# Graph products in quarters of TensorE's array, and whole transposes over all 128 rows in the place of halves

## The chip, the cores and the metric

The kernel runs on one core of one Trainium2 chip. The metric is the device time of one execution in microseconds, the median of several runs. TensorE (PE in the profile) does matmuls into PSUM; VectorE (DVE), ScalarE (ACT) and GpSimd (POOL) do the rest, and SyncE (SP) issues most DMAs. PE's array has 128 rows and 128 columns. A matmul on 64 rows or 64 columns may use a part of the array, and parts that don't overlap may work side by side. All data is fp32, and the profile shows two PE instructions for one fp32 matmul and one for a transpose.

## The reference: what is computed

`x` has 128 graphs of 64 nodes with 256 features; `adj` is one 64x64 adjacency matrix for all of them. Four graph layers follow one another, each as `x = layernorm(x + layer(x))`:

- Layer 0: the normalised adjacency is multiplied with every graph (`einsum('nm,bmd->bnd', A_hat, features)`), then two linear maps with batch norms and a relu.
- Layer 1: a Chebyshev-like product with a matrix from the adjacency and its largest eigenvalue, a linear map with layer norm and relu, attention with 4 heads inside each graph masked by the adjacency, and a feed-forward part with gelu.
- Layer 2: two graph convolutions, each `relu(einsum('ts,bsh->bth', adj, x @ W + b))`, then four LSTM passes over windows of 1 to 4 nodes, each pass writing its last state back into the nodes.
- Layer 3: graph attention with one score vector, a softmax over neighbours and a product with the values.

## The kernel before, in words

**Tiling.** The 128 graphs are cut into 16 blocks of 8 graphs. A block is one tile of 128 partitions x 1024 elements. In the token-major layout (`tm`) a partition holds one node of one graph of a pair, two graphs fill the 128 partitions, and four such pairs (`t`) with 256 features each fill the row. In the feature-major layout (`fm`) a partition is a feature, in two chunks `c` of 128, and the row holds 512 tokens. A PSUM stock `PS` has 4 such tiles of two banks each; `mem` is a stock of SBUF tiles that are taken and given back.

**Helpers on PE around the change.** `halves` is the pair of row ranges 0 to 63 and 64 to 127.

- `aggregate` (L334, matmuls at L340) is the graph product. Since the adjacency of a pair of graphs is block diagonal, it multiplies each half of the rows alone with its own 64x64 block `mT[h, h]`. The data is the stationary operand: 64 rows x 128 columns, which gives 128 features on the PSUM partitions and 64 tokens along the row. One call has 2 x 4 x 2 = 16 matmuls. Its result is feature-major.
- `to_fm` (L348) and `to_tm` (L356) turn a block from one layout to the other by PE transposes of half the rows each (L354, L361), 16 for a block. The attention weights are transposed the same way at L870.
- `part` (L320) gives each row half its own PSUM bank, so a 128-token column group lies in two places 512 elements apart. `joined` and `runs` (L324, L328) are views of PSUM and SBUF that put the two together when ScalarE or VectorE copy them out:

```
def part(ps, s, g):
    return ps[:, s * TB + g * N : s * TB + (g + 1) * N]
```

**Where they are called.** `aggregate` runs once per block in `first_block` (layer 0, L570), once in `block` (layer 1, L763) and twice in `gcn_block` (layer 2, L1317 and L1339): 64 calls. `to_tm` runs in `end_block` (L748) and in `last_block` (layer 3, L1480), `to_fm` twice in `block` (L783, L909) and once in `last_block` (L1491); with L870 that makes 96 sets of transposes. Copies out of PSUM follow each: L574 and L765, L1323, L1342 for the graph products; L751, L786, L874, L913, L1484 and L1499 for the transposes. The attention scores (L836) and the weighted values (L884) in `block` use quarters of the array, 64 rows x 64 columns, in both kernels.

**Order of the work.** The program is written by a planner, `flow` (L130). Each block's work is a generator that yields steps, `step(engine, us, ps, sl)`: the engine, a planned duration, and how many PSUM tiles and SBUF slots it takes. `flow` keeps a clock per engine and always emits the step that could begin soonest by those planned durations. So a planned duration changes no instruction, but it can change the order in which all blocks' instructions are written to each engine's queue. Within an engine the queue is worked off in that order. Up to 6 blocks of a stream are in flight, and in the middle of the run the layers overlap: LSTM units, convolutions and attention blocks of different graphs are interleaved on PE.

Of the kernel before, what the change touches and what calls it, by code (L numbers as in the profile page):

```python
# [10 lines left out]
AF = mybir.ActivationFunctionType  # L11
ALU = mybir.AluOpType
# [3 lines left out]
P = 128  # L16
B, N, D = 128, 64, 256
NBLK = 16
TB = 512
NT = 4  # L20
# [13 lines left out]
def kernel(ctx: ExitStack, tc: tile.TileContext, a: dict, out: bass.AP):  # L34
    nc = tc.nc
    V, S, G, T = nc.vector, nc.scalar, nc.gpsimd, nc.tensor
# [185 lines left out]
    H = [fm(s) for s in Hs]  # L222
# [3 lines left out]
    PS = Stock([ctile([P, NT * D], f"ps{j}", psp) for j in range(4)])  # L226
    mem = Stock([ctile([P, NT * D], f"t{j}", big) for j in range(TEMPS)])
# [15 lines left out]
    halves = slice(0, N), slice(N, P)  # L243
    for s in range(2):
        h = halves[s]
# [8 lines left out]
    ident = ctile([P, P], "ident")  # L254
# [65 lines left out]
    def part(ps, s, g):  # L320

        return ps[:, s * TB + g * N : s * TB + (g + 1) * N]

    def joined(ps, n=2 * NT):  # L324

        return ps.rearrange("p (s g e) -> p g s e", s=2, e=N)[:, :n]

    def runs(ap):  # L328

        if len(ap.shape) == 2:  # L330
            return ap.rearrange("p (g s e) -> p g s e", s=2, e=N)
        return ap.rearrange("p t (c s e) -> p (t c) s e", s=2, e=N)

    def aggregate(ps, y, mT):  # L334


        for c in range(2):
            for t in range(NT):
                for s, h in enumerate(halves):
                    T.matmul(  # L340
                        part(ps, s, c * NT + t),
                        y[h, t, c * P : (c + 1) * P],
                        mT[h, h],
                        start=True,
                        stop=True,
                    )

    def to_fm(ps, y):  # L348

        n = y.shape[1]  # L350
        for c in range(2):
            for t in range(n):
                for s, h in enumerate(halves):
                    T.transpose(part(ps, s, c * n + t), y[h, t, c * P : (c + 1) * P], ident[h, h])  # L354

    def to_tm(ps, yT):  # L356

        for t in range(yT.shape[2] // P):
            for c in range(2):
                for s, h in enumerate(halves):  # L360
                    T.transpose(part(ps, s, 2 * t + c), yT[h, c, t * P : (t + 1) * P], ident[h, h])  # L361

    def mm_fm(ps, w, yT, nk, off=0):

# [43 lines left out]
    with c0:  # L408
# [151 lines left out]
        def first_block(i):  # L560
            if i >= len(early):
                yield step("Q", 6.0, sl=1)
                xs = mem.take()
                nc.sync.dma_start(tm(mem[xs]), x_blk[i])
            else:
                xs = early[i]
            yield step("T", 0.95, ps=1, sl=1)
            ps = PS.take()
            ag = mem.take()
            aggregate(PS[ps], tm(mem[xs]), AhT)  # L570
            mem.give(xs)
            yield step("V", 1.25, ps=-1)
            aggT = fm(mem[ag])
            V.tensor_copy(runs(mem[ag]), joined(PS[ps]))  # L574
            PS.give(ps)
            for hf in range(2):
                dst = fm(Xs[i]) if hf == 0 else H[i]
                yield step("T", 3.45, ps=1)
                ps = PS.take()
                mm_fm(fm(PS[ps]), W1T, aggT, 2, off=2 * hf)  # L580
                if hf:
                    mem.give(ag)
                yield step("S", 1.3, ps=-1, waits=hf == 1)
# [136 lines left out]
        g2c = ctile([P, 2], "g2c")  # L720
        be2c = ctile([P, 2], "be2c")
# [14 lines left out]
    def end_block(i):  # L736
        x = X[i]
        yield step("Q", 6.0, sl=1)
        xin = mem.take()
        nc.sync.dma_start(tm(mem[xin]), x_blk[i])  # L740
        yield step("S", 1.4)
        for c in range(2):
            S.activation(
                H[i][:, c, :], H[i][:, c, :], AF.Identity, scale=sc2[:, c : c + 1], bias=sh2[:, c : c + 1]
            )
        yield step("T", 0.5, ps=1)
        ps = PS.take()
        to_tm(PS[ps], H[i])  # L748
        mark("h", i)
        yield step("V", 1.25, ps=-1)  # L750
        V.tensor_tensor(runs(x), joined(PS[ps]), runs(mem[xin]), ALU.add)  # L751
        PS.give(ps)
        mem.give(xin)
        yield from ln_steps_act(x)
        mark("end", i)

    def block(i):
        x = X[i]
        mark("begun", i)
        yield step("T", 0.95, ps=1, sl=1)  # L760
        ps = PS.take()
        s_xp = mem.take()
        aggregate(PS[ps], x, LnT)  # L763
# [4 lines left out]
        ps = PS.take()  # L768
# [4 lines left out]
        y = tm(mem[s_y])  # L773
# [3 lines left out]
        yield step("V", 1.25)  # L777
        V.scalar_tensor_tensor(y, y, 0.0, x, ALU.max, ALU.add)

        yield step("T", 0.5, ps=1, sl=1)  # L780
        ps = PS.take()
        s_x1 = mem.take()
        to_fm(PS[ps], y)  # L783
        yield step("S", 1.05, ps=-1)
        x1T = fm(mem[s_x1])
        S.copy(runs(mem[s_x1]), joined(PS[ps]))  # L786
        PS.give(ps)
        qk = []
        for w in (Wq, Wk):
            yield step("T", 3.45, ps=1, sl=1)  # L790
            ps = PS.take()
# [12 lines left out]
        ps = PS.take()  # L804
        s_v = mem.take()
        pv = PS[ps].rearrange("p (b u e) -> p b u e", b=8, u=2)
        for b in range(8):
            for r in range(2):
                for k in range(2):
# [4 lines left out]
                        start=(k == 0),  # L814
                        stop=(k == 1),
# [8 lines left out]
        G.tensor_tensor(y, y, row["bo"], ALU.add)  # L824


        yield step("T", 1.8, ps=1, sl=1)
        ps = PS.take()
        s_e = mem.take()
        pq = PS[ps].rearrange("p (r g m) -> p r g m", r=2, g=8)  # L830
        for t in range(NT):
            for u in range(2):
                for s in range(2):
                    b = 2 * t + s
                    for r in range(2):
# [4 lines left out]
                            start=True,  # L840
                            stop=True,
# [4 lines left out]
        e = mem[s_e].rearrange("p (g r m) -> p g r m", g=8, r=2)  # L846
# [15 lines left out]
        G.tensor_tensor(em, em, bc_last(sums, N), ALU.mult)  # L862


        yield step("T", 0.5, ps=1, sl=1)
        ps = PS.take()
        s_a = mem.take()
        for g in range(8):
            for s, h in enumerate(halves):
                T.transpose(part(PS[ps], s, g), mem[s_e][h, g * P : (g + 1) * P], ident[h, h])  # L870
        mem.give(s_e)
        yield step("S", 1.05, ps=-1)
        aT = mem[s_a].rearrange("p (g m) -> p g m", g=8)
        S.copy(runs(mem[s_a]), joined(PS[ps]))  # L874
        PS.give(ps)
        yield step("T", 1.3, ps=1, sl=1)
        ps = PS.take()
        s_o = mem.take()
        po = fm(PS[ps])
        for b in range(8):  # L880
            t, s = b // 2, b % 2
            for u in range(2):
                for r in range(2):
# [4 lines left out]
                        start=True,  # L888
                        stop=True,
# [7 lines left out]
        ps = PS.take()  # L897
# [5 lines left out]
        yield from ln_steps(y)  # L903


        yield step("T", 0.5, ps=1, sl=1)
        ps = PS.take()
        s_x2 = mem.take()
        to_fm(PS[ps], y)  # L909
        yield step("S", 1.4, ps=-1)  # L910
        x2T = fm(mem[s_x2])
        for c in range(2):
            S.activation(  # L913
                runs(mem[s_x2])[:, c * NT : (c + 1) * NT],
                joined(PS[ps])[:, c * NT : (c + 1) * NT],
                AF.Identity,
                scale=g2c[:, c : c + 1],
                bias=be2c[:, c : c + 1],
            )
        PS.give(ps)  # L920
        yield step("G", 4.7, waits=False)
# [3 lines left out]
        for hf in range(2):  # L925
            yield step("T", 3.45, ps=1, sl=1)
            ps = PS.take()
# [5 lines left out]
            for c in range(2):  # L933
                f = 2 * hf + c
# [7 lines left out]
        ps = PS.take()  # L942
        for t in range(NT):
            for k in range(4):
# [4 lines left out]
                    start=(k == 0),  # L949
                    stop=(k == 3),  # L950
# [360 lines left out]
        mem.give(s_cell)  # L1311

    def gcn_block(i):
        yield step("T", 0.95, ps=1, sl=1)
        ps = PS.take()
        s_a = mem.take()
        aggregate(PS[ps], X[i], bdAT)  # L1317
# [15 lines left out]
        PS.give(ps)  # L1333
        yield step("S", 1.05)
        S.activation(mem[s_h1], mem[s_h1], AF.Relu)
        yield step("T", 0.95, ps=1, sl=1)
        ps = PS.take()
        s_a = mem.take()
        aggregate(PS[ps], h1, bdAT)  # L1339
# [123 lines left out]
    def last_block(i, t0=0, nt=NT):  # L1463
# [9 lines left out]
        for c in range(2):  # L1473
# [1 line left out]
                hb[:, c, :].rearrange("p (b n) -> p b n", n=N),  # L1475
                hT_block(i)[:, c, :, 2 * t0 : 2 * (t0 + nt)].rearrange("p n b -> p b n"),
            )
        yield step("T", 0.5 * r, ps=1)
        ps = PS.take()
        to_tm(PS[ps], hb)  # L1480
        mem.give(s_h)
        mark("read", i)
        yield step("V", 0.1 + 1.2 * r, ps=-1)
        V.tensor_tensor(runs(x), joined(PS[ps], 2 * nt), runs(x), ALU.add)  # L1484
        PS.give(ps)
        yield from ln_steps_act(x)

        yield step("T", 0.5 * r, ps=1, sl=1)
        ps = PS.take()
        s_xT = mem.take()  # L1490
        to_fm(PS[ps], x)  # L1491


        yield step("S", 0.2 + 0.95 * r, ps=-1)
        xT = mem[s_xT][:, : 2 * nt * P]
        into = xT.rearrange("p (g f e) -> p g f e", f=4, e=N)
        pairs = joined(PS[ps], 2 * nt).rearrange("p (g f) s e -> p g f s e", f=2)
        for s, f in enumerate((slice(0, 4, 3), slice(1, 3))):
            S.copy(into[:, :, f], pairs[:, :, :, s])  # L1499
        xT = xT.rearrange("p (c k) -> p c k", c=2)  # L1500
        PS.give(ps)
        s12 = sm.tile([P, NT, 2], F32, tag="s12", name="s12")
        for t in range(0, nt, 2):
# [241 lines left out]
```

## Time and profile before

| what | value |
|---|---|
| median of 3 runs | 2440.89 us (2439.8 to 2445.77) |
| the profiled execution's own time | 2446.48 us |
| its span, first to last instruction | 2444.7 us |
| mean granted clock of TensorE | 0.979 |
| PE busy | 2323.0 us, 15636 instructions |
| PE weight loads busy | 1789.4 us |
| VectorE busy | 1255.6 us |
| ScalarE busy | 1185.4 us |
| GpSimd busy | 591.0 us |
| graph products (L340), 2048 PE instructions | 133.8 us busy |
| half transposes (L354, L361, L870), 1536 PE instructions | 73.9 us busy |

A busy time is the union of the instructions' spans on an engine. Matmuls overlap in the pipeline, so what a group costs PE is read from the start of its first instruction to the start of the next group, not from its durations. "Slot" is used below in that sense. A group's line is that of the helper, so L340 stands for all graph products.

### The profile page before, as it was taken

How to read it: one execution, taken by the hardware profiler on the slowest of the kernel's cores; microseconds unless marked ns; L12 is line 12 of the kernel's file. 1: busy time of each engine (PE TensorE's matmuls, PEld its weight loads, DVE VectorE, ACT ScalarE, POOL GpSimd, SP SyncE). 2: the span in 40 equal slices, each digit the busy share in tenths (PEclk: the TensorE clock that was granted, in tenths of full speed). 3: DMA queues.
4: the chain of work that ended last, by engine and by line, in shares of the span. 5: the costliest groups of instructions: out<-in, count | busy, mean ns of one | idle time of the engine just before them, and what ended most of it. 6: DMA issues, size and time to landing. Idle time of an engine off the chain costs nothing. (4 is left out here: it accounts for less than half of the span.)

```text
span 2444.7 us, 38027 instructions
## 1 busy us (share of the span) xinstructions
PE 2323.0 (95%) x15636; PEld 1789.4 (73%) x15636; DVE 1255.6 (51%) x2904; ACT 1185.4 (48%) x2168; POOL 591.0 (24%) x441
## 2 busy tenths in 40 slices
PE   8999878999999999999999999999999999989997
PEld 5548655767666667566677888899999888877775
DVE  4557577656447538266334344344444445455445
ACT  1248553444444343444444444444445554567676
POOL 0002134323224223233222222222221222122112
PEclk9999889999999999999999999999999999999998
DMA  5100301100000000001000000000001000101101
GB/s 154 52 1 1 106 26 40 36 9 10 1 10 10 18 10 10 1 18 44 9 27 1 27 18 1 1 18 1 1 1 35 1 10 9 35 27 44 52 18 53
DMA packets 42622, 57.74 MB, mean 24 GB/s; under 512 B 6224, under 2 KB 35536, under 8 KB 42448
## 3 DMA queue, kind: packets, MB, share of 16 engines
q1 hardware_dynamic: 41344, 54.22, 6.8%
q8 instruction: 123, 2.02, 0.4%
q10 hardware_dynamic: 1104, 1.08, 0.1%
q14 instruction: 51, 0.42, 0.1%
HBM read 38.52 MB, written 16.78 MB: 23 GB/s over the span
## 5 line engine op out<-in xcount | busy, mean ns | idle before, releaser
L1134 PE MATMUL ps<-x,x 128*128 128x256 f32 x864 | 212.9, 381 | 1.6 <-DVE x L1193 1.0
L1134 PEld LDWEIGHTS ps<-x,x 128*128 128x128 f32 x864 | 160.6, 190 | 25.2 <-issue 2.0
L1134 PE MATMUL ps<-t,x 128*128 128x256 f32 x704 | 170.0, 380 | 0.0
L314 ACT ACTIVATE x<-x,ln_nm,ln_rs 128x256 f32<-128x256 f32 x188 | 99.6, 592 | 122.9 <-DVE ln_nm L311 122.9
L1134 PEld LDWEIGHTS ps<-t,x 128*128 128x128 f32 x704 | 132.9, 190 | 18.9 <-issue 0.8
L308 POOL TENSOR_TENSOR ln_rs<-ln_rs,neghalf 128x4 f32<-128x4 f32 (+1 forms) x72 | 69.9, 970 | 213.0 <-DVE ln_rs L274 200.7
L367 PE MATMUL ps<-t,W1T 128*128 128x512 f32 x256 | 116.5, 603 | 0.0
L1210 ACT ACTIVATE t<-t,bih 128x512 f32<-128x512 f32 (+2 forms) x63 | 40.4, 641 | 105.7 <-DVE t L1200 101.0
L294 POOL TENSOR_TENSOR ln_rs<-ln_rs,neghalf 128x4 f32<-128x4 f32 x32 | 36.6, 1143 | 224.4 <-DVE ln_rs L274 224.4
L1062 PE MATMUL ps<-h,wL 128*128 128x192 f32 (+2 forms) x456 | 90.4, 352 | 0.0
L1062 PE MATMUL ps<-h,x 128*128 128x256 f32 x384 | 86.8, 380 | 1.5 <-ACT t L1074 1.5
L1193 DVE COPY t<-ps 128x256 f32<-128x256 f32 (+2 forms) x63 | 23.4, 371 | 123.9 <-PE ps L1134 123.9
L272 DVE BATCH_NORM_STATS2 ln_st<-x 128x6 f32<-128x256 f32 x224 | 85.4, 403 | 0.4
L367 PEld LDWEIGHTS ps<-t,W1T 128*128 128x128 f32 x256 | 47.4, 194 | 49.4 <-issue 49.4
L1062 PEld LDWEIGHTS ps<-h,wL 128*128 128x128 f32 x456 | 70.1, 190 | 16.8 <-issue 15.8
L1062 PEld LDWEIGHTS ps<-h,x 128*128 128x128 f32 x384 | 72.7, 190 | 12.3 <-ACT t L1074 1.6
L1074 ACT ACTIVATE t<-ps,bih 128x512 f32<-128x512 f32 (+3 forms) x108 | 63.6, 639 | 34.3 <-PE ps L1062 34.2
L1062 PE MATMUL ps<-t,wL 128*128 128x512 f32 x168 | 73.7, 594 | 1.3 <-ACT t L1360 0.7
L1074 ACT ACTIVATE x<-ps,bih 128x512 f32<-128x512 f32 (+3 forms) x84 | 48.9, 634 | 52.3 <-PE ps L1062 52.1
L273 DVE BATCH_NORM_AGGREGATE ln_mv<-ln_st 128x2 f32<-128x6 f32 x448 | 71.6, 167 | 0.0
L1210 ACT ACTIVATE x<-x,bih 128x512 f32<-128x512 f32 (+2 forms) x64 | 41.8, 653 | 57.6 <-DVE x L1200 57.4
L1062 PE MATMUL ps<-x,wL 128*128 128x512 f32 x144 | 62.9, 593 | 0.0
(712 smaller groups left out, 5760.6 us busy)
## 6 DMA issues: line engine op xcount, KB each, us to landing
t<-in_x_dram SPq DMA_DIRECT2D x26, 512.0 KB, 4.2
xd<-x SPq DMA_DIRECT2D x16, 512.0 KB, 2.6
x<-xd SPq DMA_DIRECT2D x6, 512.0 KB, 3.4
out_dram<-x SPq DMA_DIRECT2D x6, 512.0 KB, 3.0
h<-in_x_dram SPq DMA_DIRECT2D x5, 512.0 KB, 3.9
wL<-in_L_gnn_Wih_dram SPq DMA_DIRECT2D x2, 1024.0 KB, 5.1
x<-in_L_gnn_Whh_dram SPq DMA_DIRECT2D x2, 1024.0 KB, 6.2
t<-xd SPq DMA_DIRECT2D x4, 512.0 KB, 3.6
```

Of the source, the lines that this page charges most:

```text
L272: V.bn_stats(st[:, t, :], y[:, t, :])
L273: V.bn_aggr(mv[:, t, :], st[:, t, :])
L294: G.tensor_tensor(rs, rs, neghalf[:, :NT], ALU.pow)
L308: G.tensor_tensor(rs, rs, neghalf[:, :n], ALU.pow)
L314: S.activation(y[:, t, :], y[:, t, :], AF.Identity, scale=rs[:, t : t + 1], bias=nm[:, t : t + 1])
L367: T.matmul(ps[:, c, :], w[:, k, (off + c) * P : (off + c + 1) * P], yT[:, k, :], start=(k == 0), stop=(k == nk - 1),)
L1062: T.matmul(spread(fm(PS[ps])[:, j, :n], q), WL[p][0][:, k, m], x_of(0, q)[:, k], start=(k == 0), stop=(k == 1),)
L1074: S.activation(of(sl)[:, j], fm(PS[ps])[:, j, :n], AF.Tanh if g == 2 else AF.Sigmoid, bias=bias(g, c))
L1134: T.matmul(dst, WS[p][name](k, g), y[:, k], start=first and k == 0, stop=k == 1, skip_group_check=not first)
L1193: V.tensor_copy(y[:, 1, :], v[:, 0, :])
L1210: S.activation(of(act[g])[:, 0], of(act[g])[:, 0], f, bias=bias(g, 0))
```

## The change

`aggregate` splits each matmul in two by its stationary columns: 64 rows x 64 columns, which write 64 PSUM partitions each, at the same PSUM places as before, so its results are copied out with the same views. One call has 32 matmuls in the place of 16.

`to_fm`, `to_tm` and the attention transposes work on all 128 rows and 128 columns at once with the whole identity: 8 transposes for a block in the place of 16. Their results lie contiguous in PSUM, so the copies that follow use plain views. In `last_block` the swap of the two halves of every second pair, which the old views held, becomes three copies in the place of two.

The planned durations of the graph products go from 0.95 to 1.15 us, of the scores from 1.8 to 1.15, of the weighted values from 1.3 to 1.15, and of a set of transposes from 0.5 to 0.9; that of the copy in `last_block` goes from 0.2 + 0.95 r to 0.3 + 1.1 r, where r is the part of a block that is worked on.

```diff
         for c in range(2):
             for t in range(NT):
-                for s, h in enumerate(halves):
-                    T.matmul(
-                        part(ps, s, c * NT + t),
-                        y[h, t, c * P : (c + 1) * P],
-                        mT[h, h],
...
+                for f, to in enumerate(halves):
+                    for s, h in enumerate(halves):
+                        T.matmul(
+                            part(ps, s, c * NT + t)[to],
+                            y[h, t, c * P + f * N : c * P + (f + 1) * N],
+                            mT[h, h],
...
     def to_fm(ps, y):
-        n = y.shape[1]
         for c in range(2):
-            for t in range(n):
-                for s, h in enumerate(halves):
-                    T.transpose(part(ps, s, c * n + t), y[h, t, c * P : (c + 1) * P], ident[h, h])
+            for t in range(y.shape[1]):
+                T.transpose(ps[:, c, t * P : (t + 1) * P], y[:, t, c * P : (c + 1) * P], ident)
 
     def to_tm(ps, yT):
-        for t in range(yT.shape[2] // P):
+        for t in range(ps.shape[1]):
             for c in range(2):
-                for s, h in enumerate(halves):
-                    T.transpose(part(ps, s, 2 * t + c), yT[h, c, t * P : (t + 1) * P], ident[h, h])
+                T.transpose(ps[:, t, c * P : (c + 1) * P], yT[:, c, t * P : (t + 1) * P], ident)
...
-            yield step("T", 0.95, ps=1, sl=1)
+            yield step("T", 1.15, ps=1, sl=1)
             ps = PS.take()
             ag = mem.take()
             aggregate(PS[ps], tm(mem[xs]), AhT)
...
-        yield step("T", 0.5, ps=1)
-        ps = PS.take()
-        to_tm(PS[ps], H[i])
+        yield step("T", 0.9, ps=1)
+        ps = PS.take()
+        to_tm(tm(PS[ps]), H[i])
         mark("h", i)
         yield step("V", 1.25, ps=-1)
-        V.tensor_tensor(runs(x), joined(PS[ps]), runs(mem[xin]), ALU.add)
+        V.tensor_tensor(x, tm(PS[ps]), tm(mem[xin]), ALU.add)
...
-        S.copy(runs(mem[s_x1]), joined(PS[ps]))
+        S.copy(mem[s_x1], PS[ps])
...
-        yield step("T", 1.8, ps=1, sl=1)
+        yield step("T", 1.15, ps=1, sl=1)
...
         for g in range(8):
-            for s, h in enumerate(halves):
-                T.transpose(part(PS[ps], s, g), mem[s_e][h, g * P : (g + 1) * P], ident[h, h])
+            T.transpose(PS[ps][:, g * P : (g + 1) * P], mem[s_e][:, g * P : (g + 1) * P], ident)
...
-        yield step("T", 1.3, ps=1, sl=1)
+        yield step("T", 1.15, ps=1, sl=1)
...
-        yield step("S", 0.2 + 0.95 * r, ps=-1)
-        xT = mem[s_xT][:, : 2 * nt * P]
-        into = xT.rearrange("p (g f e) -> p g f e", f=4, e=N)
-        pairs = joined(PS[ps], 2 * nt).rearrange("p (g f) s e -> p g f s e", f=2)
-        for s, f in enumerate((slice(0, 4, 3), slice(1, 3))):
-            S.copy(into[:, :, f], pairs[:, :, :, s])
-        xT = xT.rearrange("p (c k) -> p c k", c=2)
+        yield step("S", 0.3 + 1.1 * r, ps=-1)
+        xT = fm(mem[s_xT])[:, :, : nt * P]
+        pairs, into = (ap.rearrange("p c (u e k) -> p c u e k", e=2, k=P) for ap in (px, xT))
+        S.copy(into[:, :, :, 0], pairs[:, :, :, 0])
+        for h in range(2):
+            S.copy(into[:, :, :, 1, halves[1 - h]], pairs[:, :, :, 1, halves[h]])
```

More of the change, by code (lines that the diff above doesn't have):

```diff
@@ L338, in aggregate @@
             for t in range(NT):
-                for s, h in enumerate(halves):
-                    T.matmul(
-                        part(ps, s, c * NT + t),
-                        y[h, t, c * P : (c + 1) * P],
-                        mT[h, h],
-                        start=True,
-                        stop=True,
-                    )
+                for f, to in enumerate(halves):
[4 more added lines that the diff above has]
+                            mT[h, h],
+                            start=True,
+                            stop=True,
+                        )
     def to_fm(ps, y):
-        n = y.shape[1]
         for c in range(2):
-            for t in range(n):
-                for s, h in enumerate(halves):
-                    T.transpose(part(ps, s, c * n + t), y[h, t, c * P : (c + 1) * P], ident[h, h])
+            for t in range(y.shape[1]):
+                T.transpose(ps[:, c, t * P : (t + 1) * P], y[:, t, c * P : (c + 1) * P], ident)
     def to_tm(ps, yT):
-        for t in range(yT.shape[2] // P):
+        for t in range(ps.shape[1]):
             for c in range(2):
-                for s, h in enumerate(halves):
-                    T.transpose(part(ps, s, 2 * t + c), yT[h, c, t * P : (t + 1) * P], ident[h, h])
+                T.transpose(ps[:, t, c * P : (c + 1) * P], yT[:, c, t * P : (t + 1) * P], ident)
     def mm_fm(ps, w, yT, nk, off=0):
@@ L759, in block @@
         mark("begun", i)
-        yield step("T", 0.95, ps=1, sl=1)
+        yield step("T", 1.15, ps=1, sl=1)
         ps = PS.take()
@@ L778, in block @@
         V.scalar_tensor_tensor(y, y, 0.0, x, ALU.max, ALU.add)
-        yield step("T", 0.5, ps=1, sl=1)
+        yield step("T", 0.9, ps=1, sl=1)
         ps = PS.take()
         s_x1 = mem.take()
-        to_fm(PS[ps], y)
+        to_fm(fm(PS[ps]), y)
         yield step("S", 1.05, ps=-1)
         x1T = fm(mem[s_x1])
-        S.copy(runs(mem[s_x1]), joined(PS[ps]))
+        S.copy(mem[s_x1], PS[ps])
         PS.give(ps)
@@ L862, in block @@
         G.tensor_tensor(em, em, bc_last(sums, N), ALU.mult)
-        yield step("T", 0.5, ps=1, sl=1)
+        yield step("T", 0.9, ps=1, sl=1)
         ps = PS.take()
@@ L873, in block @@
         aT = mem[s_a].rearrange("p (g m) -> p g m", g=8)
-        S.copy(runs(mem[s_a]), joined(PS[ps]))
+        S.copy(mem[s_a], PS[ps])
         PS.give(ps)
-        yield step("T", 1.3, ps=1, sl=1)
+        yield step("T", 1.15, ps=1, sl=1)
         ps = PS.take()
@@ L903, in block @@
         yield from ln_steps(y)
-        yield step("T", 0.5, ps=1, sl=1)
+        yield step("T", 0.9, ps=1, sl=1)
         ps = PS.take()
         s_x2 = mem.take()
-        to_fm(PS[ps], y)
+        to_fm(fm(PS[ps]), y)
         yield step("S", 1.4, ps=-1)
@@ L913, in block @@
             S.activation(
[L914 to L918, printed above, removed]
+                x2T[:, c, :], fm(PS[ps])[:, c, :], AF.Identity, scale=g2c[:, c : c + 1], bias=be2c[:, c : c + 1]
             )
@@ L1313, in gcn_block @@
     def gcn_block(i):
-        yield step("T", 0.95, ps=1, sl=1)
+        yield step("T", 1.15, ps=1, sl=1)
         ps = PS.take()
@@ L1335, in gcn_block @@
         S.activation(mem[s_h1], mem[s_h1], AF.Relu)
-        yield step("T", 0.95, ps=1, sl=1)
+        yield step("T", 1.15, ps=1, sl=1)
         ps = PS.take()
@@ L1477, in last_block @@
             )
-        yield step("T", 0.5 * r, ps=1)
+        yield step("T", 0.9 * r, ps=1)
         ps = PS.take()
-        to_tm(PS[ps], hb)
+        px = tm(PS[ps])[:, :nt, :]
+        to_tm(px, hb)
         mem.give(s_h)
@@ L1483, in last_block @@
         yield step("V", 0.1 + 1.2 * r, ps=-1)
-        V.tensor_tensor(runs(x), joined(PS[ps], 2 * nt), runs(x), ALU.add)
+        V.tensor_tensor(x, px, x, ALU.add)
         PS.give(ps)
         yield from ln_steps_act(x)
-        yield step("T", 0.5 * r, ps=1, sl=1)
+        yield step("T", 0.9 * r, ps=1, sl=1)
         ps = PS.take()
         s_xT = mem.take()
-        to_fm(PS[ps], x)
-        yield step("S", 0.2 + 0.95 * r, ps=-1)
-        xT = mem[s_xT][:, : 2 * nt * P]
-        into = xT.rearrange("p (g f e) -> p g f e", f=4, e=N)
-        pairs = joined(PS[ps], 2 * nt).rearrange("p (g f) s e -> p g f s e", f=2)
-        for s, f in enumerate((slice(0, 4, 3), slice(1, 3))):
-            S.copy(into[:, :, f], pairs[:, :, :, s])
-        xT = xT.rearrange("p (c k) -> p c k", c=2)
+        px = fm(PS[ps])[:, :, : nt * P]
+        to_fm(px, x)
+        yield step("S", 0.3 + 1.1 * r, ps=-1)
[4 more added lines that the diff above has]
+            S.copy(into[:, :, :, 1, halves[1 - h]], pairs[:, :, :, 1, halves[h]])
         PS.give(ps)
```

## The prediction, made before the result was known

> **What bounds the kernel.** I read the page's busy shares first, then a table of stages, then the PE's timeline one group of instructions at a time.
>
> ```profile
> PE 2323.0 (95%) x15636; PEld 1789.4 (73%) x15636; DVE 1255.6 (51%) x2904; ACT 1185.4 (48%) x2168; POOL 591.0 (24%) x441
> ...
> PE   8999878999999999999999999999999999989997
> ...
> PEclk9999889999999999999999999999999999999998
> ```
>
> TensorE is busy 95% of the span, the next engine 51%. A busy PE alone proves little, since matmul ends are modelled, so the stages (columns: sum, then PE, weight loads, VectorE, ScalarE, GpSimd, clock, DMA):
>
> ```profile
> 0.00:160.00 160.00, 151.96 (x828) 91.16 (x829) 76.48 (x158) 38.33 (x60) 2.51 (x15) 1.00 0.28 79
> ...
> 280.00:500.00 220.00, 190.57 (x1828) 135.88 (x1829) 155.24 (x404) 112.21 (x162) 78.53 (x53) 0.88 0.15 46
> 500.00:1100.00 600.00, 580.21 (x4697) 389.45 (x4696) 326.04 (x719) 258.03 (x325) 177.41 (x107) 0.99 0.03 10
> ...
> 2200.00:2445.00 245.00, 210.45 (x1468) 169.83 (x1467) 121.47 (x452) 169.73 (x387) 46.89 (x62) 0.94 0.13 42
> ```
>
> The changed groups lie at 0 to 160 (layer 0), 280 to 1400 (layers 1 and 2) and 1900 to 2445 (layer 3); 1400 to 1900 has none. PE sets the pace everywhere except at 280 to 500 and after 2200, where it idles some 30 and 35 us and the clock falls to 0.88 and 0.94. Now what one group costs, as start, duration, line:
>
> ```profile
> 434.16 2.00 PE L340 MATMUL ps<-bdAT,x 64*128 64x64 f32 x32
> 436.00 0.67 PE L870 MATMUL ps<-ident,t 64*128 64x64 f32 x16
> 436.50 0.67 PE L361 MATMUL ps<-ident,h 64*128 64x64 f32 x16
> 437.09 1.95 PE L1015 MATMUL ps<-av,h 128*128 128x1 f32 x16
> ```
>
> The same with full-array neighbours, later on:
>
> ```profile
> 1378.44 1.03 PE L1134 MATMUL ps<-x,x 128*128 128x256 f32 x4
> 1379.40 2.00 PE L340 MATMUL ps<-bdAT,x 64*128 64x64 f32 x32
> 1381.33 2.86 PE L1134 MATMUL ps<-x,x 128*128 128x256 f32 x12
> ```
>
> And the attention scores, which use quarters of the array already:
>
> ```profile
> 414.17 1.16 PE L836 MATMUL ps<-t,h 64*64 64x64 f32 x64
> 415.27 0.71 PE L354 MATMUL ps<-ident,t 64*128 64x64 f32 x16
> ```
>
> Read the starts, since ends overlap. A graph product (L340) is 16 matmuls, two instructions each in fp32, and holds PE 1.84 us up to a neighbour in the same array mode, 1.93 us up to a full-array one. The attention scores (L836) are already 32 products of 64x64 in the array's quarters: 64 instructions in 1.10 us. A set of half transposes (L870, L361) is 16 single instructions: 0.50 us, or 0.59 when a full-array matmul follows.
>
> **What the Trainium skill says.** "TensorE: Matmul & The Clock Gate", section "LDWEIGHTS (loading the stationary operand)": a load takes time by its columns, not its rows. The trace agrees (minimum/median/maximum ns):
>
> ```profile
> L340 PEld LDWEIGHTS ps<-bdAT,x x640: 182/188/188, 434.2 to 1381.1; 64*128 64x128 f32 x160
> L340 PE MATMUL ps<-bdAT,x x640: 272/272/320, 434.2 to 1381.1; 64*128 64x64 f32 x160
> ...
> L836 PEld LDWEIGHTS ps<-h,t x384: 129/135/135, 330.1 to 1079.2; 64*64 64x64 f32 x192
> L836 PE MATMUL ps<-h,t x384: 218/218/268, 330.1 to 1079.3; 64*64 64x64 f32 x192
> ```
>
> Half the columns take 53 ns off a load. L340 streams only 64 columns per 128 loaded, so loads pace it. "TensorEngine Tiling (Array Packing)", section "Key Properties": changing the tiling mode drains the array. The trace agrees: four 128x256 matmuls from 1378.44 should end their turn at 1379.30 (each 0.215 us; L1134 repeats it everywhere), but L340 starts at 1379.40; and leaving costs the 0.09 between 1.84 and 1.93. The same page, "Gotcha 2: Feature Incompatibilities", says that column tiling excludes fp32 transpose mode, so transposes cannot be quartered too; no run here shows it. The clock page, "Terms", calls transpose mode four times faster for fp32: the trace has one instruction per transpose for two per matmul, and a 128-column load at 139 ns instead of 188; it does not show whether the moving side also doubles its rate.
>
> **The change, part by part.** *Graph products.* 64 calls (16 in layer 0, 16 and 32 in layers 1 and 2). Each becomes 64 instructions of 64x64, four tiles in turn, each row group writing its own PSUM bank: L836's pattern. Its 1.10 us replaces 1.93: -0.83. I take off the switching overhead inside both (0.09 out, about 0.05 for the exposed first load): 1.79 to 0.95, -0.84 x 64 = -53.8 us. Bounds: no gain if quarters do not run four at once here (0); -0.90 at best.
>
> *Transposes.* 16 calls at layer 1's entry, 48 in its blocks, 32 in layer 3 (counting two half blocks as one): 96. Sixteen instructions at 0.031 us in two concurrent row halves (0.50) become eight over all rows, each loading 128 columns and streaming 128. No such instruction is in the trace. Lower bound: 0.062 each, the pace of a pair of halves, if 128 columns stream in the time of the load: 0.50 per call, no cost. Upper bound with the load hidden: the ordinary rate. Matmul durations are 275 ns for 128 columns, 380 for 256, 593 for 512, or 0.83 ns per column; a half transpose's 223 for 64 columns lies on that same line. So 128 columns stream in 107 ns; with 5 of overhead (0.215 us per 128x256 is 2 over its 213; two-tile and four-tile turns show 3 to 9) 0.112, eight 0.90. I take this: +0.40 x 96 = +38.4 us. If loads could not hide at all, 0.165 each, 1.32 per call; but the present pace already hides them.
>
> *Mode switches.* Whole transposes share the full-array mode of most matmuls. Following PE's instructions in order, the mode changes 340 times now; with today's order and the new modes it would change 231 times. A switch is worth 0.12 us (0.10 entering, 0.05 first load, 0.09 leaving, over two): -109 x 0.12 = -13.1 us.
>
> *Evacuation.* Copies out of PSUM become contiguous. Strided ones (L786, L874) take 1.01 us, contiguous ones (L798) 1.00; the adds at L751 and L774 are 1.21 and 1.22: nothing. Layer 3's copy of x (L1499) goes from two instructions of 0.58 to one of 0.58 and two of about 0.39: +0.2 us on ScalarE for some 20 blocks, 4 us, largely under PE; 1 us on the path.
>
> *Order.* The new step costs reorder the whole written program: graph products 0.95 to 1.15, scores 1.8 to 1.15, weighted values 1.3 to 1.15, transposes 0.5 to 0.9. Beside the trace (1.9, 1.1, 1.1, 0.5 now) the new figures fit the new code better than the old fit the old. PE has about 120 us of idle time. Bounds: -15 if half the idle time of 280 to 500 closes, +30 if it doubles; I take +3. No wait, DMA or buffer is added, and nothing is moved past a queue.
>
> By stage: layer 0, 16 x -0.84 = -13.4, all kept, with PE at 95% and ScalarE, which waits for it, at 24%. 280 to 1400: 48 x -0.84 + 64 x 0.40 - 53 x 0.12 = -21.1, of which I keep 19, since at 280 to 500 PE waits for others. Layer 3: 32 x 0.40 - 56 x 0.12 + 1 = +7.1. Order +3. Sum -22.3. The profiled execution took 2446.5 (span 2444.7 and 1.8 around it), so 2424 for it; that execution is 0.2% over the median of the runs, 2440.9, which gives **2418 us**.
>
> **Rivals.** *Transposes stream at one column per cycle*: the 38.4 goes, -61 in place of -22.3: about 2382 with some loss to waits. For it, the weight load already runs at the double rate; against it, the 223 ns on the ordinary line. *The order eats the gain*: gaps at 280 to 500 and after 2200 grow, and each long one costs half-clock time besides, as PEclk shows there now; another 20 us of idle gives about 2438. For it: these stages already wait. Against it: 500 to 1100 is 97% PE and no idle gap there can shrink or grow by much. *Slower: the quarters do not run four at once in the graph product.* Both column tiles of a row group stream the same 64x64 adjacency block and write neighbouring partitions of one bank; should they take turns, four take 0.112 instead of 0.058, a call stays at 1.79, and the rest of the sum is left, +38.4 - 13.1 + 1 + 3: about 2470. It decides above (38.4 - 13.1) / 64 = 0.40 us of lost gain per call, 1.4 us per product. Against it stands L836 with the same tiles, though its moving data differ between column tiles.
>
> **How the numbers follow.** Likeliest case 0.64 (its own range 2403 to 2433), fast transposes 0.13, order eats it 0.14, no concurrency 0.09. A measurement of this kernel tells about 0.3% (7 us) from no change. Faster: 0.60 of the first, 0.13, and 0.02 of the third: 0.75. Slower: 0.09, 0.04 of the third and 0.01: 0.14. Same: 0.11. The range, 2376 to 2441, leaves out the no-concurrency case, the worst of the order case and the far end of fast transposes.
>
> **What the changed profile would show.** L340-type groups of 64 instructions with slots near 1.1 us; transposes of 128x128 near 0.9 us per eight; layer 0 shorter by 13 us; half-clock stretches no more than now. I am wrong if the eight take 0.5 or 1.3 us, if the quarters take over 1.4, or if idle PE time grows by more than 15 us.

## The result, and the profile after

The changed kernel takes 2407.65 us (median of four runs, 2406.91 to 2409.44). The ratio to the kernel before is 0.9863, with an interval of 0.9846 to 0.9880: faster by 33 us, where 22 were forecast. The profiled execution took 2409.44 us, its span is 2407.7, so 37.0 under the span before.

The page of the changed kernel, busy times and the rows of PE and its clock:

```profile
PE 2287.2 (95%) x16916; PEld 1759.9 (73%) x16916; DVE 1287.7 (53%) x2904; ACT 1187.4 (49%) x2189; POOL 591.7 (25%) x441
...
PE   8999788999989999999999999999999999998997
...
PEclk9999899999999999999999999999999999999998
```

PE still fills 95% of a shorter span. It has 1280 matmul instructions more: 2048 for the products, less 768 for the transposes. The same stages as before (sum, PE, weight loads, VectorE, ScalarE, GpSimd, clock, DMA):

```profile
0.00:160.00 160.00, 143.42 (x1354) 77.68 (x1354) 81.19 (x170) 41.81 (x65) 3.53 (x16) 0.97 0.29 79
280.00:500.00 220.00, 197.17 (x1986) 138.04 (x1990) 144.91 (x347) 116.24 (x165) 72.00 (x46) 0.95 0.10 33
500.00:1100.00 600.00, 574.40 (x5358) 382.80 (x5349) 364.09 (x778) 256.44 (x324) 194.94 (x115) 0.98 0.03 10
2200.00:2408.00 208.00, 181.60 (x1135) 146.15 (x1133) 106.88 (x404) 152.82 (x361) 42.96 (x58) 0.97 0.14 46
```

The clock at 280 to 500 rose from 0.88 to 0.95. PE is busy for less of the first 160 us and of 500 to 1100 than before. Now the groups. PE's timeline (start, duration, line), first a graph product between full-array matmuls, then a set of whole transposes, then the two next to each other:

```profile
1293.24 1.16 PE L341 MATMUL ps<-bdAT,x 64*64 64x64 f32 x64
1294.33 2.86 PE L1127 MATMUL ps<-x,x 128*128 128x256 f32 x12
```

```profile
595.82 1.04 PE L867 MATMUL ps<-ident,t 128*128 128x128 f32 x8
596.79 3.44 PE L808 MATMUL ps<-wA,t 128*64 128x128 f32 x58
```

```profile
996.02 1.16 PE L341 MATMUL ps<-bdAT,h 64*64 64x64 f32 x64
997.11 1.10 PE L867 MATMUL ps<-ident,h 128*128 128x128 f32 x8
998.13 1.16 PE L881 MATMUL ps<-t,x 64*64 64x64 f32 x64
```

From start to start a product takes 1.09 us (1.93 before). Eight transposes take 0.97 up to a group in another mode; between full-array neighbours they take 0.87, 0.109 each:

```profile
564.92 1.04 PE L353 MATMUL ps<-ident,x 128*128 128x128 f32 x8
565.79 3.62 PE L377 MATMUL ps<-wA,h 128*128 128x256 f32 x16
```

The instructions themselves (minimum/median/maximum ns), products and the transposes of layer 1's inputs:

```profile
L341 PEld LDWEIGHTS ps<-bdAT,x x1408: 129/135/228, 421.6 to 1294.1; 64*64 64x64 f32 x176
L341 PE MATMUL ps<-bdAT,x x1408: 218/218/366, 421.6 to 1294.2; 64*64 64x64 f32 x176
```

```profile
L353 PEld LDWEIGHTS ps<-ident,t x176: 138/141/231, 298.8 to 2246.0; 128*128 128x128 f32 x176
L353 PE MATMUL ps<-ident,t x176: 271/273/477, 298.8 to 2246.1; 128*128 128x128 f32 x176
```

The products look like the attention scores did. A whole transpose loads at the fast rate (141 ns) but lasts 273 ns, like the ordinary 128-column matmul instruction of 275.

**Accounts of PE's time.** For the comparisons below I cut PE's time from its first to its last matmul in four: *work*, each instruction at its own undisturbed pace at full clock; *switches* of array mode at 0.117 us; *half clock*, what the throttle adds to the work; *idle*, the rest. This is worked out from the starts of all matmuls in each trace, so it is an estimate: how a half-clock stretch is charged to its instructions can move differences between runs by up to some 7 us from one of the last two columns to the other, and smaller ones are not read singly. Some 17 us of every span lie before the first and after the last. The kernel before, run beside each batch, had medians of 2440 to 2446 us, so the ratios compare across batches better than the times do.

| run | ratio to before, 95% | span | work | switches | half clock | idle |
|---|---|---|---|---|---|---|
| before | | 2444.7 | 2197 | 40 (340) | 42 | 149 |
| the change | 0.9863 (0.9846 to 0.9880) | 2407.7 | 2178 | 28 (240) | 37 | 148 |
| q_old_order | 0.9923 (0.9909 to 0.9937) | 2421.5 | 2143 | 40 | 44 | 178 |
| w_old_order | 1.0005 (0.9996 to 1.0014) | 2446.0 | 2233 | 28 | 39 | 129 |
| both_old_order | 0.9907 (0.9892 to 0.9921) | 2416.3 | 2178 | 27 | 41 | 155 |
| new_order_only | 1.0008 (0.9998 to 1.0017) | 2439.1 | 2197 | 39 | 46 | 140 |
| q_halves_new_order | 0.9880 (0.9864 to 0.9895) | 2409.8 | 2143 | 41 | 44 | 165 |
| q_halves | 0.9955 (0.9939 to 0.9970) | 2427.0 | 2143 | 39 | 48 | 180 |
| two_tiles | 0.9966 (0.9955 to 0.9976) | 2432.8 | 2226 | 28 | 30 | 131 |
| full_array | 0.9924 (0.9907 to 0.9942) | 2426.5 | 2230 | 18 | 30 | 132 |
| products_twice | 1.0228 (1.0214 to 1.0242) | 2493.4 | 2238 | 28 | 37 | 174 |
| transposes_twice | 1.0102 (1.0087 to 1.0117) | 2465.7 | 2262 | 29 | 29 | 129 |
| after_lag | 0.9933 (0.9919 to 0.9947) | 2424.9 | 2178 | 26 | 42 | 161 |
| q_halves_lag | 0.9904 (0.9891 to 0.9917) | 2414.9 | 2143 | 40 | 44 | 171 |

From before to after the work falls by 19 (products -55, transposes +36), the switches by 12, half clock and idle together by 6: 37 in all. So far the work and the switches are as in the forecast's sum. The experiments show that it isn't that simple.

### The profile page after: what moved, and what is told of

It reads as the page before. It is cut to its first block, busy times and chain, and to the rows that moved or that the text cites. A ratio compares the mean times of both kernels' runs of the same rounds, so it can differ in the third digit from the quotient of the medians.

```text
span 2407.7 us, 40603 instructions
## 1 busy us (share of the span) xinstructions
PE 2287.2 (95%) x16916; PEld 1759.9 (73%) x16916; DVE 1287.7 (53%) x2904; ACT 1187.4 (49%) x2189; POOL 591.7 (25%) x441
## 4 chain that ended last, share of the span: by engine, by line
PE 60%; DVE 16%; ACT 7%; POOL 3%; issue 2%; POOLq 0%; ACTq 0%; DVEq 0%
PE ps L1127 26%; PE ps L1055 11%; PE ps L365 7%; PE ps L377 4%; PE ps L938 4%; DVE ln_st L272 3%; ACT x L314 2%; PE ps L808 2%; POOL ln_rs L308 1%; PE ps L1507 1%; DVE x L300 1%; PE ps L341 1%; DVE ln_mv L273 1%; PE ps L353 1%; DVE ln_nm L311 1%
## 5 line engine op out<-in xcount | busy, mean ns | idle before, releaser
L1127 PE MATMUL ps<-x,x 128*128 128x256 f32 x928 | 225.0, 380 | 0.7 <-DVE t L1195 0.7
L1127 PEld LDWEIGHTS ps<-x,x 128*128 128x128 f32 x928 | 173.5, 190 | 24.9 <-issue 1.6
L314 ACT ACTIVATE x<-x,ln_nm,ln_rs 128x256 f32<-128x256 f32 x212 | 112.3, 592 | 133.3 <-DVE ln_nm L311 131.9
L1127 PEld LDWEIGHTS ps<-t,x 128*128 128x128 f32 x672 | 126.4, 190 | 17.1 <-DVE x L1195 0.8
L1055 PE MATMUL ps<-h,wL 128*128 128x192 f32 (+2 forms) x480 | 103.9, 371 | 4.8 <-ACT h L1353 4.8
L272 DVE BATCH_NORM_STATS2 ln_st<-x 128x6 f32<-128x256 f32 x260 | 99.7, 403 | 0.4
L1067 ACT ACTIVATE t<-ps,bih 128x512 f32<-128x512 f32 (+3 forms) x98 | 57.2, 634 | 55.8 <-PE ps L1055 55.1
L1186 DVE COPY x<-ps 128x256 f32<-128x256 f32 (+2 forms) x69 | 26.1, 378 | 108.4 <-PE ps L1127 107.6
L365 PE MATMUL ps<-t,wA 128*128 128x512 f32 x160 | 76.8, 626 | 5.5 <-ACT t L784 5.5
L1193 DVE TENSOR_TENSOR x<-ps,x 128x512 f32<-128x512 f32 (+2 forms) x69 | 41.4, 602 | 53.0 <-PE ps L1127 43.6
```

The costliest lines, as they stand in the source:

```text
L272: V.bn_stats(st[:, t, :], y[:, t, :])
L314: S.activation(y[:, t, :], y[:, t, :], AF.Identity, scale=rs[:, t : t + 1], bias=nm[:, t : t + 1])
L365: T.matmul(ps[:, c, :], w[:, k, (off + c) * P : (off + c + 1) * P], yT[:, k, :], start=(k == 0), stop=(k == nk - 1),)
L1055: T.matmul(spread(fm(PS[ps])[:, j, :n], q), WL[p][0][:, k, m], x_of(0, q)[:, k], start=(k == 0), stop=(k == 1),)
L1067: S.activation(of(sl)[:, j], fm(PS[ps])[:, j, :n], AF.Tanh if g == 2 else AF.Sigmoid, bias=bias(g, c))
L1127: T.matmul(dst, WS[p][name](k, g), y[:, k], start=first and k == 0, stop=k == 1, skip_group_check=not first)
```

## Experiments: the parts one at a time

**Quarters alone, in the order of before.**

```diff
 # the kernel before; its planned durations and half transposes stay
-                for s, h in enumerate(halves):
-                    T.matmul(part(ps, s, c * NT + t), y[h, t, c * P : (c + 1) * P], mT[h, h], ...
+                for f, to in enumerate(halves):
+                    for s, h in enumerate(halves):
+                        T.matmul(part(ps, s, c * NT + t)[to], y[h, t, c * P + f * N : c * P + (f + 1) * N], mT[h, h], ...
```

> The kernel before with its graph products in quarters, and nothing else: halves for the transposes, and the planned durations, so the order of the steps, of before. Theory (prices of the parts add up): 64 products save 0.84 us each, 54 us; the switches of mode between products and half transposes, which shared a mode until now, cost 2 to 4 us back: some 2390 us, 49 to 52 under before. Rival (the gain came from the new order of the steps): well under half of the 33 us that the change brought, 2425 or more. Rival (quarters take turns, not side by side): 2440 or more.

Measured: 2422.97 us, 18 under before by the medians. The work fell by 55 as priced, but by the account idle time rose by some 30. Neither theory's number: the saving is real on PE, and about half of it turns into waiting. The trace shows two kinds. PE's waits for results of ScalarE and VectorE, summed over the trace, grew from 111 to 128 us. And a second kind, which the kernel before has not at all, takes 6 us in seven stops: PE stops inside a burst with nothing to wait for, as here in its timeline (the last bracket is the idle time before and its releaser; "issue" means none that the profile shows):

```profile
724.81 0.65 PE L341 MATMUL ps<-bdAT,x 64*64 64x64 f32 x32
725.28 1.11 PE L885 MATMUL ps<-x,x 64*64 64x64 f32 x64
726.29 1.49 PE L341 MATMUL ps<-LnT,x 64*64 64x64 f32 x82
729.01 0.92 PE L341 MATMUL ps<-LnT,x 64*64 64x64 f32 x46 [1.23 <-issue]
```

**Whole transposes alone, in the order of before.**

```diff
 # the kernel before, with to_fm, to_tm, the attention transposes and the copies after them as in the change
-                for s, h in enumerate(halves):
-                    T.transpose(part(ps, s, c * n + t), y[h, t, c * P : (c + 1) * P], ident[h, h])
+                T.transpose(ps[:, c, t * P : (t + 1) * P], y[:, t, c * P : (c + 1) * P], ident)
```

> The kernel before with whole transposes, and nothing else: graph products in row halves, planned durations and order of before. Theory: 96 sets of 8 at 0.109 us in place of 16 at 0.031 cost 0.37 us each, 36 us, and fewer switches of mode give back about 10: slower by 24 to 28 us, near 2466. Rival (whole transposes cost nothing where PE waits for others, or the saved switches pay for them): within 8 us of before.

Measured: 2443.03 us, ratio 1.0005, no difference. The rival had it. The work rose by the 36 that I priced, the switches fell by 11.5, half clock by 3, and the remaining 20 us came out of idle time: waits for ScalarE and VectorE shrank from 111 to 93 us. Why the waits gave up all of it here is not shown. With the transposes doubled (below) they gave up about a quarter.

**Both, in the order of before; and the new order alone.**

```diff
 # both_old_order: the changed kernel, each planned duration as before, such as
-        yield step("T", 0.9, ps=1, sl=1)
+        yield step("T", 0.5, ps=1, sl=1)
 # new_order_only: the kernel before, each planned duration as in the change
-        yield step("T", 0.5, ps=1, sl=1)
+        yield step("T", 0.9, ps=1, sl=1)
```

> The changed kernel's instructions written in the order of before: the code of the change with all planned durations of before. Theory: the sum of the parts, about 30 us under before, 2410, within 6 us of the changed kernel, since the order is worth little. Rival (the new order is a good part of the gain): 2420 or more, that is 12 us or more over the changed kernel.

> The kernel before, instructions unchanged, with the planned durations of the change: the order of the steps alone. Theory: within 8 us of before, 2432 to 2448. Rival (order matters): faster by 12 us or more. If it is slower by more than 8, the change gained in spite of its order, and the parts are worth more than their sum here.

Measured: 2419.03 and 2442.54 us. With the old order the change brings 22 us by the medians, with its own 33. The new order without the new instructions brings nothing (ratio 1.0008). So the parts are not a sum: -18, +2 and +1.5 alone, -33 together. Two thirds of the gain come with the instructions, one third from an order that does nothing for the old ones. My theory for both_old_order missed (2413.7 was its limit, 2419 was measured), and its rival's 2420 was closer; the theory for new_order_only held.

## Experiments: could half transposes be kept?

The halves do less PE work, so quarters with halves ought to beat both kernels.

```diff
 # q_halves_new_order: the kernel before, with the quarters, and every planned duration of the change
 # q_halves: the same instructions, with durations that suit them
-        yield step("T", 0.9, ps=1, sl=1)
+        yield step("T", 0.6, ps=1, sl=1)
```

> The changed kernel with its whole transposes put back into halves, the planned durations and so the order of the steps as the change has them. The PE work falls by 36 us and some 100 switches of mode, 12 us, come back: 24 us less for PE. Theory (with this order PE sets the pace, as the 33 us of the change showed): 15 us or more of it are seen, 2392 or less. Rival (the stage of layers 1 and 2 is held by the chain through the other engines, so less PE work turns into idle PE time, as it did for the quarters alone in the old order): within 8 us of the changed kernel, 2400 to 2416.

> The same instructions as the run before (quarters and half transposes), ordered by planned durations that suit them: graph products, scores and weighted values 1.15, transposes 0.6. Theory (a planned duration near the real one lets the order hide more): at or under the run before, 2380 to 2392. Rival (the order is chance, worth some 10 us either way): no closer to the sum than the run before, or slower than it.

Measured: 2414.16 us (ratio 0.9880, beside 0.9863 for the change: intervals overlap) and 2432.44 (0.9955). Halves take 36 us of work off the changed kernel, and nothing comes of it: the switches return 13, half clock and idle together 24. That is the whole-transposes experiment backwards, with the same outcome, and the rival's. The order with the truer durations was the worse by 18 us, so a truer plan is no better plan here, as its rival said.

Read together, the ratios tell what each part is worth. The quarters alone bring 18 us. The new order brings 10 to 11 more wherever there are quarters (q_old_order to q_halves_new_order 0.9923 to 0.9880, both_old_order to the change 0.9907 to 0.9863), and nothing without them. The whole transposes bring some 4 us beside quarters, in either order, and each time the intervals overlap: no gain is shown for them. Whole transposes in the new order without quarters were not run.

> The changed kernel, instructions unchanged, with the planner told that results arrive later: 0.5 us after a PE step in place of 0.2, 0.15 after others in place of 0.06, so that it puts more other work between a step and its use. Theory (the idle PE time comes of the written order, where a step stands too soon after the one it needs): idle PE time falls, 3 to 15 us under the changed kernel. Rival (it comes of the chain's length and the few blocks in flight): within 3 us of it or slower.

> Quarters and half transposes with the planned durations of the change and the same later arrivals in the planner. Theory (idle comes of the order): the 24 us less PE work show at last, at or under the changed kernel, 2385 to 2405. Rival: 2410 or more, as without.

```diff
-LAG, LAG_T = 0.06, 0.2
+LAG, LAG_T = 0.15, 0.5
```

Measured: 2426.95 (0.9933) and 2417.25 (0.9904). Telling the planner of later results made the changed kernel slower by 17 us by the ratios, with 13 more idle, and did nothing for the other (0.9880 before it). My theory that slack in the order would lower the idle time fell. What these runs show is that the same instructions in another order differ by up to some 20 us. What it would take to find an order with less waiting stays open. No version that I ran beats the change.

## Experiments: what makes the quarters fast

**Two tiles at a time.**

```diff
-        for c in range(2):
-            for t in range(NT):
-                for f, to in enumerate(halves):
+        for f, to in enumerate(halves):
+            for c in range(2):
+                for t in range(NT):
```

> The changed kernel with the loop over the two column halves of a graph product outermost: the same 64 instructions, planned durations and order of the steps, but for 32 instructions on end only two tiles of the array are in use. Theory (four tiles side by side make the gain; two tiles give a pair in 0.058 us): a product takes about 1.86 us in place of 0.95, 0.9 x 64 = 58 us more PE work, of which at least half shows: 2436 to 2466. Rival (the shorter loads alone make the gain, the turn of the tiles is of no account): within 5 us of the changed kernel.

Measured: 2435.34 us (0.9966), just under the theory's range (2436 to 2466) and far from the rival. PE's timeline of this kernel, one product, then two on end:

```profile
62.48 1.91 PE L341 MATMUL ps<-AhT,t 64*64 64x64 f32 x64
64.32 0.49 PE L497 MATMUL ps<-eM 128*128 128x128 f32 x2
...
99.92 3.43 PE L341 MATMUL ps<-AhT,t 64*64 64x64 f32 x128
103.28 0.49 PE L497 MATMUL ps<-eM 128*128 128x128 f32 x2
```

One product takes 1.84 us between full-array matmuls, where the same 64 instructions with four tiles in turn take 1.09. Two on end take 3.36, so the second adds 1.52; with four tiles it adds 0.93 (two take 2.02). The loads are as short as in the change (135 ns). So the concurrency of the column tiles is the gain; a short load in itself is little of it. Of 48 us more work (64 x 0.75) 25 show, by the spans.

**No tiles at all.**

```diff
-                for f, to in enumerate(halves):
-                    for s, h in enumerate(halves):
-                        T.matmul(part(ps, s, c * NT + t)[to], y[h, t, c * P + f * N : c * P + (f + 1) * N], mT[h, h], ...
+                T.matmul(fm(ps)[:, c, t * P : (t + 1) * P], y[:, t, c * P : (c + 1) * P], mT, start=True, stop=True)
```

> The changed kernel with each graph product on the whole array: 8 matmuls over 128 rows with the block-diagonal 128x128 adjacency, which multiplies by the zeros between the two graphs too. Theory (loads of 128 columns pace a product, so splitting by rows alone bought nothing): 16 instructions at 0.109 to 0.112 us, 1.75 to 1.79 us, as the row halves took, and no switch of mode: 0.8 x 64 = 51 less 120 switches at 0.12 = 14, so 37 us more PE work than the changed kernel; 2425 to 2445, no slower than the kernel before. Rival (row halves ran side by side to some profit): 2455 or more.

Measured: 2424.82 us (0.9924), at the lower edge of the theory (2425 to 2445): under the kernel before, while multiplying twice as much, half of it zeros. Its timeline:

```profile
101.27 3.74 PE L339 MATMUL ps<-AhT,t 128*128 128x128 f32 x32
104.84 0.39 PE L489 MATMUL ps<-eM 128*128 128x128 f32 x2
```

Two products in 3.57 us, 1.79 each: exactly what the row halves took before (1.79), without their switches. Rows alone bought nothing. For the row halves the loads of 128 columns are the likely pace: half transposes, of the same shape but with a load of 139 ns for 188, took 0.031 each where these took 0.056. Over the whole array load and stream can't be told apart here: whole transposes, with loads of 141 ns for 192, take the same 0.109 to 0.112 per instruction, so the stream of 128 columns alone would do.

**Each group twice.**

```diff
 # products_twice
+        for _ in range(2):
             for c in range(2):
 # transposes_twice, at each of the three transposes
                 T.transpose(ps[:, c, t * P : (t + 1) * P], y[:, t, c * P : (c + 1) * P], ident)
+                T.transpose(ps[:, c, t * P : (t + 1) * P], y[:, t, c * P : (c + 1) * P], ident)
```

> The changed kernel with every graph product issued twice over, into the same place, planned durations and order unchanged: 64 x 0.93 = 60 us more PE work and no other. Theory (idle PE time in the stage of layers 1 and 2 is what gives way, since PE there waits for results of the other engines): about half of it shows, 25 to 35 us over the changed kernel, 2433 to 2443, and idle PE time falls by the rest. Rival (PE sets the pace): 50 us or more.

> The changed kernel with every whole transpose issued twice, planned durations and order unchanged: 96 x 0.87 = 84 us more PE work. Theory (as for the products: about half shows): 35 to 50 us over the changed kernel. Rival (transposes lie where PE waits anyway and cost nothing, as the whole transposes alone seemed to): under 20 us. Rival (PE sets the pace): 70 us or more.

Measured: 2497.78 us (1.0228) and 2467.18 (1.0102). Of 84 us more transposes, 58 show by the spans: between the theory (35 to 50) and the rival that PE sets the pace (70); idle and half-clock time give the other 26. Sixty more of products cost 86: more than they take, and more than the theory's 25 to 35. The timeline of products_twice at the start says why:

```profile
8.26 5.32 PE L342 MATMUL ps<-AhT,t 64*64 64x64 f32 x219
15.39 0.80 PE L342 MATMUL ps<-AhT,t 64*64 64x64 f32 x37 [1.81 <-issue]
16.12 0.49 PE L498 MATMUL ps<-eM 128*128 128x128 f32 x2
16.54 1.55 PE L342 MATMUL ps<-AhT,t 64*64 64x64 f32 x89
20.21 0.81 PE L342 MATMUL ps<-AhT,t 64*64 64x64 f32 x39 [2.12 <-issue]
```

PE stops for 2 us, twice, waiting for nothing that the profile knows. The first of these two stops comes after its 223rd matmul and the second after its 351st, and the others keep to steps of 127 or 128 or a multiple (606, 989, 1116, 1244). Such stops, counted by the profile's view of PE's waits (us in all, times, longest), are 18, for 21.5 us:

```profile
PE ps L342 <- issue: 19.8, 17, 2.1
PE ps L882 <- issue: 1.7, 1, 1.7
```

The pages' rows of the instruction queue, of before, then of products_twice:

```profile
q8 instruction: 123, 2.02, 0.4%
```

```profile
q8 instruction: 164, 2.69, 0.5%
```

There are 41 more packets (of 16 KB) for 5376 more matmuls: one packet holds 131 of them with their loads, by this count. In all 18 stops of products_twice PE goes on 1.24 to 1.55 us after the latest of these packets landed, and in all 7 of q_old_order 1.23 to 1.50 us after (one landed at 727.51, and PE went on at 729.01, above). No two packets land closer than 3.39 us in either trace, while four tiles in turn use 128 matmul instructions in 1.87 us. So PE had probably used up what it had, and the next piece came too late. The timing and the spacing of 25 stops say so; no run changed the supply itself.

## Why the prediction was right, and where it was not

- *Graph products, -53.8.* Right as PE work: -55, at 1.09 us as the scores had shown. The rival of quarters taking turns fell: the four run at once though both column tiles stream the same adjacency block, as two_tiles shows by contrast (1.84).
- *Transposes, +38.4.* Right as PE work: eight take 0.87 where I had 0.90, +36. Reading 223 ns for 64 columns on the line of ordinary matmuls was sound: whole ones last 273. The rival of one column per cycle fell: of the four times that the Trainium skill gives fp32 transpose mode ("TensorE: Matmul & The Clock Gate", "Terms"), the trace shows the faster load and one instruction in place of two, but not a faster stream. In all it is about twice as fast, not four times (0.109 us, where the two instructions of an ordinary matmul took 2 x 0.112 in full_array), and the measurement decides.
- *Switches, 109 fewer at 0.12.* 100 fewer, 12 us, for 13.
- *Evacuation, nothing.* In agreement; ScalarE's busy time rose by 2.0 us. VectorE's rose by 32, but that goes with the order: 1284 us in new_order_only, where the copies are the old ones, and 1255 in both_old_order, where they are the new ones.
- *By stage: PE sets the pace, so nearly all of the net is kept.* This is the step that failed, though its total came out. Layer 0 kept 10.9 of 13.4 (its second linear map, L606, L608 before, began at 161.4 us for 172.3), and PE idles 17 of the first 160 us there, where it idled 8. My list of stages where PE idles also left out 160 to 280 and 1900 to 2200, with 12 and 13 us. In layers 1 and 2 PE's busy share of 97% hid that its short waits give and take: taken alone, 55 us less work brought 18, and 36 us more cost nothing. I netted the two on PE before asking what waits do with each. Taken one to one, the saving was overrated by some 35 us and the cost, with its fewer switches, by some 23, and most of the error cancelled: without its order term the forecast was -25, and both_old_order measured -22. That the sum came out so near is luck as much as reckoning.
- *Order, +3.* Wrong in sign and size for these instructions: some -11, by both_old_order. For the old instructions it was +1.5. Its bounds of -15 and +30 held. These 14 us are more than the whole of the 10 us between forecast and measurement; the rest of the sum was 3 or 4 us too hopeful.
- *Half clock.* I gave it no gain. The granted clock rose from 0.88 to 0.95 at 280 to 500 and fell from 1.00 to 0.97 in layer 0; over the span it went from 0.979 to 0.982, worth 5 us by the account, which is no more than the account can tell.
- *Rivals.* "The order eats the gain" is the one whose mechanism is real: other orders of the same instructions lost 17 us (after_lag) and 18 (q_halves).

## What to carry to other kernels

Price a PE group from start to start, in its own array mode with the switches on both sides, and look for an existing group of the same shape: the scores' 1.09 us told the products' time to the hundredth. But don't bank PE time one to one because PE is 95% busy: in an in-order queue with short waits everywhere, a saving of 55 us brought 18 alone and an added 36 cost nothing. Test each part alone in a fixed order before calling it the cause. Count instructions too: bursts of tiny matmuls seem to outrun the supply of instructions.

## What the runs showed of the hardware that was not expected

- A 64-row, 128-column fp32 product on row halves and the same product on the whole array with half zeros take the same 1.79 us; 64x64 quarters four in turn take 0.93 to 0.94. Between full-array neighbours, switches included, four in turn take 1.09 and two in turn 1.84.
- An fp32 transpose of 128x128 loads fast (141 ns, where an ordinary load takes 190) but takes its turn every 109 ns, about as long as each of the two instructions of an ordinary matmul of 128 columns (112, in full_array).
- Dense 64x64 matmuls stop for 0.2 to 2.1 us at multiples of about 128 matmuls and go on some 1.2 to 1.6 us after an instruction packet of 16 KB has landed: no such stop in the kernel before, 0.9 us in the change, 6 with quarters and halves in the old order, 21.5 with the products doubled.
